# Sixteen pairs of expert visits done 256 columns wide in a mixture-of-experts loop

## Chip, cores and metric

The kernel runs on one core of a Trainium2 chip. The metric is the device time of one execution in microseconds, median of several runs. The engines are named as in the profile: PE (TensorE matmul), PEld (its weight loads), DVE (VectorE), ACT (ScalarE), POOL (GpSimd) and SP (SyncE, which here only issues DMAs).

## What is computed

Two decoder layers over 8 sequences of 128 tokens with 256 features, each with an attention, a cross attention and a feed-forward part, and a layer norm of the sum after each. The part that matters here is the last one, a mixture of 64 experts of which every token uses 8. With 1,024 tokens that makes 8,192 pairs of a token and an expert:

```python
x = hidden_states.reshape(-1, HIDDEN)
logits = jnp.einsum('th,eh->te', x, gate_w)
probs = jax.nn.softmax(logits, axis=-1)
topk_w, topk_idx = jax.lax.top_k(probs, TOP_K)
...
def step(acc, inp):
    w13_e, w2_e, c = inp
    g = x @ w13_e[:INTER].T
    u = x @ w13_e[INTER:].T
    h = jax.nn.silu(g) * u
    o = h @ w2_e.T 
    return (acc + c[:, None] * o, None)
```

`g` and `u` are 128 wide, `o` 256. All of it is fp32. The kernel computes `o` for chosen pairs alone.

## The kernel before

**Order of the pairs.** The pairs are sorted by expert, so that each expert owns a run of columns. `cols` holds the features of the sorted pairs, 128 partitions by 2 halves by 64 blocks of 128 columns and two blocks more. An expert with n pairs takes ceil(n / 128) *visits*, each of 128 columns from a start that is known only at run time. There are at most 127 visits (`NV`); the program has a shorter arm for up to 104 (`FEW`) and chooses by a counted value (L1212 to L1219).

**The routing ahead of the loop.** `choose` takes the best 8 of 64 per token into a mask. `place` counts the pairs of each expert by a matmul with ones (L928 to L930), copies the counts to 128 columns (L935), and multiplies them with a triangle of ones (`before`) to get each expert's first slot (`base`, L937). That is added to the slot numbers (L943). Later, visits per expert are counted (`full`, L991 to L993), summed up to the first visit of each expert (`first`, L994 to L997), and turned into two rows of `visits`: the expert of each visit and its first column (L1049 to L1058). A third row tells the arm. Beside this, DVE and PE turn the slots into one-hot matrices and out of them into `tok_i`, the token of each sorted pair (`locate` and L1029 to L1063). The loop's first gathers wait for `tok_i`.

**The loop, `run_visits`.** One step does one visit v. The order of PE and of POOL is the program's (a manual schedule); the orders of DVE, ACT and SP are the scheduler's.

- `hidden(v)`: PE reads the visit's first column into a register (`begins`, L1119), then 4 fp32 matmuls against gate and up weights, which the profile shows as 8 records of 128 columns (L1150). ACT takes silu of one half (L1158), DVE multiplies with the other (L1160).
- `turn(g)`: PE transposes a gathered block of 128 pairs in two matmuls (L1128) into one of the two PSUM buffers of `ps_tr`, and DVE copies it into `cols` (L1129). `turned(step)` says how many blocks are turned after a step: step + 3 + step // 4, so every fourth step turns two.
- `down(v - 2)`: 2 fp32 matmuls, 4 records (L1167), and ACT copies the result to `cols` over columns that are no longer needed (L1170).
- `fetch(v + 8)`: SP loads the visit's expert, 384 KB, into a ring of 9 tiles (L1138).
- `gather`: POOL gathers blocks by `tok_i`, four ahead of the turned ones, into 6 buffers (L1104).
- `turn_back(g)`: from step 43 on PE transposes a finished block (L1177), DVE copies it (L1179) and POOL scatters it to `pair_rows` in HBM (L1180).
- `weight(b)` and `spread(b)`: DVE work for the tail, in the program every twelfth step; the scheduler puts most of it early.

A block may be used by a visit only once its copy is in `cols`. The visit's first column is at most 128 v, so visit v waits for blocks up to number v.

**The tail.** Eight loads of 1 MB bring the scattered rows back, PE and DVE sum the eight experts of each token with their weights, and a layer norm ends the kernel.

Of the kernel before, what the change touches and what calls it, by code (L numbers as in the profile page):

```python
# [9 lines left out]
F32 = mybir.dt.float32  # L10
# [4 lines left out]
ALU = mybir.AluOpType  # L15
# [22 lines left out]
FEW = 104  # L38
FAR = 65536.0
# [20 lines left out]
def decoder_kernel(ctx: ExitStack, tc: tile.TileContext, i, out):  # L60
# [594 lines left out]
    blks_16 = rp.tile([P, NG, TOP], F16, name="blks_16")  # L655
    comb = rp.tile([P, B, NE], F32, name="combine")
# [20 lines left out]
    def make_constants():  # L677
# [14 lines left out]
        nc.gpsimd.iota(blks_16, pattern=[[1, NG], [0, TOP]], base=0, channel_multiplier=0, allow_small_or_imprecise_dtypes=True)  # L692
        nc.gpsimd.memset(seen[:, 0, :], 0.0)
# [89 lines left out]
    with (  # L783
# [136 lines left out]
        def place(st, b, par):  # L920
# [42 lines left out]
        counts = rp.tile([NE, 2], F32, name="counts")  # L963
        counts_w = rp.tile([NE, P], F32, name="counts_w")
# [34 lines left out]
    lead = rp.tile([NE, 1], F32, name="lead")  # L999
    nc.scalar.activation(lead, first[:, 1:2], AF.Identity, bias=first[:, 0:1], scale=-float(P))  # L1000
    done = rp.tile([NE, 1], F32, name="done")
    nc.scalar.activation(done, first[:, 1:2], AF.Identity, bias=counts[:, 1:2], scale=1.0)
    past = rp.tile([NE, P], F32, name="past")
    nc.gpsimd.tensor_scalar(past, iota[:NE], done, None, ALU.is_ge)
    during = rp.tile([NE, P], F32, name="during")
    nc.gpsimd.tensor_scalar(during, iota[:NE], first[:, 1:2], None, ALU.is_ge)
# [19 lines left out]
    with tc.tile_pool(name="onehot", bufs=3) as op, tc.manual_schedule(engines={nc.vector.engine}):  # L1026
        pn = ps_mm("pair_in").rearrange("p (k g) -> p k g", k=TOP)
        locate(0, 2)
        for b in range(B):  # L1029
# [16 lines left out]
            if b == 0:  # L1046

                px = ps_o("expert_of")[:1, :P]
                nc.tensor.matmul(px, ones[:NE, :1], past, start=True, stop=True)  # L1049
# [6 lines left out]
                nc.gpsimd.tensor_copy(visits[:, 2, :], by_visit[:, 0])  # L1056
# [18 lines left out]
    wring = loop.enter_context(tc.tile_pool(name="wring", bufs=9, side="right"))  # L1075
# [35 lines left out]
    def run_visits(arm, count):  # L1111


# [17 lines left out]
        def fetch(v):  # L1131
# [10 lines left out]
            ws[v] = w  # L1142

        def hidden(v):
            o = begins(v, nc.tensor.engine, fed)
            ps = ps_mm(f"moe_gu_{arm}_{v}")[:, :D].rearrange("p (a t) -> p a t", a=2)
            for a in range(2):
                for k in range(2):
                    at = k * D + a * P
                    mm = nc.tensor.matmul(  # L1150
                        ps[:, a, :], ws[v][:, at : at + P], cols[:, k, bass.ds(o + P, P)],
# [5 lines left out]
            s = mp.tile([P, P], F32, tag="s", name=f"moe_s_{arm}_{v}")  # L1157
            nc.scalar.activation(s, ps[:, 0, :], AF.Silu)  # L1158
            hid = mp.tile([P, P], F32, tag="hid", bufs=4, name=f"moe_h_{arm}_{v}")
            nc.vector.tensor_tensor(hid, ps[:, 1, :], s, ALU.mult)  # L1160
            hs[v] = hid

        def down(v):
            ps = ps_o(f"moe_o_{arm}_{v}")[:, :D].rearrange("p (c t) -> p c t", c=2)
            for c in range(2):
                at = 2 * D + c * P
                nc.tensor.matmul(ps[:, c, :], ws[v][:, at : at + P], hs[v], start=True, stop=True)  # L1167
# [147 lines left out]
```

## Time and profile before

| | |
|---|---|
| median of 3 runs | 881.4 us (881.01 to 885.09) |
| the profiled execution | 886.73 us, span 884.9 us |
| PE busy in the span | 804.7 us (91%) |
| weight loads | 537.0 us (61%) |
| DVE, ACT, POOL busy | 459.7, 289.8, 231.7 us |
| weight loads from HBM in the loop | 104 of 384 KB |
| gathers and scatters | 64 and 64 indirect DMAs |
| first matmul of visit 0 | 639.1 us after the start |
| last start of a down matmul | 843.4 us |

The page gives shares over the whole span. The loop is some 204 us of it, and it has two parts: in the first, blocks are gathered and turned; in the second (about 727 us on), finished blocks are turned back and scattered. The clock that was granted to PE is 1.00 in nearly all of the loop. Records of matmuls overlap, since their ends are modelled; what one costs is read from the distance of starts.

### The profile page before, as it was taken

To read this page: it belongs to the slowest core of one execution; us is meant where nothing else is said; L and a number is where in the kernel's file an instruction comes from. 1 tells how busy PE (TensorE), PEld (TensorE's weight loads), DVE (VectorE), ACT (ScalarE), POOL (GpSimd) and SP (SyncE) were. 2 spreads that over 40 slices of the span, in tenths; PEclk is the share of its full clock that TensorE was granted. 3 is DMA by queue.
4 is the path that set the end of the run, shared out by engine and by line. 5 is a ranking of instruction groups with operands and counts; after the bars stand their busy time and mean duration, and the time that the engine had idled before them with its cause. 6 is when DMAs were issued, how large, how long until landed. Compare 5 with 4: busy or idle time off the path is not lost. (4 is left out here: it accounts for less than half of the span.)

```text
span 884.9 us, 14249 instructions
## 1 busy us (share of the span) xinstructions
PE 804.7 (91%) x4568; PEld 537.0 (61%) x4568; DVE 459.7 (52%) x1280; ACT 289.8 (33%) x994; POOL 231.7 (26%) x321
## 2 busy tenths in 40 slices
PE   7998986999999999999999999996588888999946
PEld 3555553567455558655557755554488877888834
DVE  1899976323544442344444477665795333334326
ACT  2567752221333330133330133332232332333302
POOL 0011113123300000000006121101566655555524
PEclk9999996999999999999999999997599999999979
DMA  6500010730000000000001000000579987989656
GB/s 186 160 1 25 1 49 1 262 119 0 1 0 1 0 1 1 1 0 1 1 1 48 1 7 8 13 13 13 196 227 284 289 273 229 296 294 301 200 205 262
DMA packets 39731, 87.80 MB, mean 99 GB/s; under 512 B 6433, under 2 KB 16193, under 8 KB 38753
## 3 DMA queue, kind: packets, MB, share of 16 engines
q1 hardware_dynamic: 32288, 68.88, 24.0%
q0 software_dynamic: 6144, 16.79, 5.6%
q10 hardware_dynamic: 1216, 1.13, 0.4%
q8 instruction: 41, 0.67, 0.3%
q14 instruction: 42, 0.34, 0.1%
HBM read 76.29 MB, written 10.49 MB: 98 GB/s over the span
## 5 line engine op out<-in xcount | busy, mean ns | idle before, releaser
L228 ACT ACTIVATE l_e<-l_s,nm_l 128x128 f32<-128x128 f32 x256 | 90.2, 370 | 88.7 <-DVE nm_l L225 88.6
L1150 PE MATMUL moe_gu_few<-cols,w_few 128*128 (+1 forms) x832 | 114.6, 281 | 3.7 <-issue 2.3
L1150 PEld LDWEIGHTS moe_gu_few<-cols,w_few 128*128 128x128 f32 x832 | 102.7, 194 | 10.6 <-issue 9.2
L1180 POOL DMA_INDIRECT pair_rows<-moe_os_few,pairs x64 | 63.1, 986 | 55.2 <-DVE moe_os_few L1179 42.9
L1104 POOL DMA_INDIRECT xg_few<-x_rows,tok_i x60 | 62.2, 1037 | 30.8 <-issue 11.9
L1167 PE MATMUL moe_o_few<-moe_h_few,w_few 128*128 128x128 f32 x416 | 63.9, 277 | 0.0
L748 PE MATMUL l_q<-xT_l1a,w_qkv 128*128 128x512 f32 x128 | 60.2, 593 | 0.0
L748 PE MATMUL l_k<-xT_l1a,w_qkv 128*128 128x512 f32 x128 | 60.2, 592 | 0.0
L748 PE MATMUL l_v<-xT_l1a,w_qkv 128*128 128x512 f32 x128 | 60.1, 592 | 0.0
L235 DVE TENSOR_SCALAR l_e<-l_e,inv_l 128x128 f32<-128x128 f32 x256 | 59.3, 295 | 1.2
L851 ACT ACTIVATE y_e<-y_sT 128x512 f32<-128x512 f32 x64 | 33.0, 604 | 81.5 <-PE y_sT L844 48.8
L1170 ACT COPY cols<-moe_o_few 128x256 f32 (+1 forms) x104 | 38.8, 373 | 57.5 <-PE moe_oT_few L1177 21.6
L731 DVE TENSOR_TENSOR l_vs<-l_c,l_vs 128x512 f32<-128x512 f32 x32 | 22.1, 692 | 67.4 <-PE l_c L730 67.4
L711 PE MATMUL l_y<-w_o,l_vs 128*128 128x256 f32 x256 | 56.9, 381 | 0.0
L1158 ACT ACTIVATE moe_s_few<-moe_gu_few 128x128 f32<-128x128 f32 x104 | 29.0, 280 | 80.4 <-PE moe_gu_few L1150 44.8
L1167 PEld LDWEIGHTS moe_o_few<-moe_h_few,w_few 128*128 128x128 f32 x416 | 55.2, 193 | 0.0
L711 PEld LDWEIGHTS l_y<-w_o,l_vs 128*128 128x128 f32 x256 | 48.1, 190 | 9.8 <-issue 2.8
L228 ACT ACTIVATION_READ_ACCUMULATOR l_e<-l_s,nm_l 128x1 f32 x256 | 53.2, 208 | 0.0
L1160 DVE TENSOR_TENSOR moe_h_few<-moe_gu_few,moe_s_few 128x128 f32<-128x128 f32 x104 | 29.8, 287 | 42.2 <-ACT moe_s_few L1158 23.8
L1129 DVE COPY cols<-moe_xT_few 128x256 f32<-128x256 f32 x64 | 26.5, 418 | 47.1 <-PE moe_o_few L1167 23.7
L225 DVE TENSOR_REDUCE nm_l<-l_s 128x4 f32<-128x512 f32 x64 | 43.1, 684 | 10.0 <-PE l_s L763 8.1
L756 ACT COPY l_vs<-l_v 128x512 f32<-128x512 f32 x32 | 18.7, 585 | 78.5 <-PE l_v L748 78.5
(266 smaller groups left out, 1355.8 us busy)
## 6 DMA issues: line engine op xcount, KB each, us to landing
w_few<-in_experts SPq DMA_DIRECT2D x104, 384.0 KB
z<-pair_rows SPq DMA_DIRECT2D x7, 1024.0 KB
w_qkv<-in_w_qkv SPq DMA_DIRECT2D x8, 768.0 KB
w_o<-in_w_o SPq DMA_DIRECT2D x1, 2048.0 KB
xT<-in_xT SPq DMA_DIRECT2D x2, 512.0 KB
x<-in_x SPq DMA_DIRECT2D x4, 256.0 KB
cx<-in_ctx SPq DMA_DIRECT2D x1, 1024.0 KB
q_up<-in_up_qT SPq DMA_DIRECT2D x4, 256.0 KB
```

Of the source, the lines that this page charges most:

```text
L225: nc.vector.tensor_reduce(nm, s, AX.X, ALU.max, negate=True)
L228: nc.scalar.activation(e[:, a, :], s[:, a, :], AF.Exp, bias=nm[:, a : a + 1], scale=1.0, accum_out=sums[:, a : a + 1],)
L235: nc.vector.tensor_scalar(e[:, a, :], e[:, a, :], inv[:, a : a + 1], None, ALU.mult)
L711: nc.tensor.matmul(py[:, :D], scaled[b // 4, m][:, b % 4 * S : (b % 4 + 1) * S], w_o[:, m, :], start=(m == 0), stop=(m == L1_HEADS - 1),)
L748: nc.tensor.matmul(ps, w_qkv[:, k, c, n, :], xT[h][:, k, :], start=(k == 0), stop=(k == 1))
L851: nc.scalar.activation(e, tiles[j], AF.Exp)
L1104: nc.gpsimd.indirect_dma_start(out=x, out_offset=None, in_=xd, in_offset=bass.IndirectOffsetOnAxis(ap=tok_i[:, g : g + 1], axis=0), bounds ...
L1150: mm = nc.tensor.matmul(ps[:, a, :], ws[v][:, at : at + P], cols[:, k, bass.ds(o + P, P)], start=(k == 0), stop=(k == 1),)
L1160: nc.vector.tensor_tensor(hid, ps[:, 1, :], s, ALU.mult)
L1167: nc.tensor.matmul(ps[:, c, :], ws[v][:, at : at + P], hs[v], start=True, stop=True)
L1170: cp = nc.scalar.copy(cols[:, :, bass.ds(o, P)], ps)
L1180: inst = nc.gpsimd.indirect_dma_start(out=zd, out_offset=bass.IndirectOffsetOnAxis(ap=pairs[:, g : g + 1], axis=0), in_=o, in_offset=None, ...
```

## The change

Experts whose number of visits is even are sorted ahead of the others. The first 32 visits are then 16 pairs of one expert each, and a pair is done as one unit: one load of weights, matmuls, silu, product and copy of 256 columns in place of 128. Visits 32 to 103 are units of one visit as before. So the arm has 88 units and 88 loads of weights where it had 104.

For the new order, the experts stand twice on 128 partitions: partitions 0 to 63 count an expert if its number of visits is even, 64 to 127 if it is odd (`even`, `alt`, `keep`). The counts are taken twice, `full` and `first` move ahead into `place`, and `base` is made of `first` by way of `twice`, which folds the two halves. `step_of` undoes the doubling when the expert of a visit is counted. The arm is chosen by two conditions: at least 16 pairs and at most 104 visits. The ring of weights has 8 tiles in place of 9 and is filled 7 units ahead in place of 8; the buffers for silu are 2 of double width in place of 3. In a unit of two visits the loop turns the blocks of both steps one after the other.

```diff
 FEW = 104
+DOUBLES = 16
...
+        for half in range(2):
+            rows = slice(NE * half, NE * (half + 1))
+            nc.gpsimd.memset(even[rows], 1.0 - half)
+            by_two = alt.rearrange("p (j two) -> p j two", two=2)
+            for two in range(2):
+                nc.gpsimd.memset(by_two[rows, :, two], 1.0 if half != two else -1.0)
+        nc.gpsimd.tensor_tensor(twice, ident[:, :NE], ident[:, NE:], ALU.add)
+        nc.gpsimd.tensor_scalar(step_of, ident[:, NE - 1 : NE], -float(NE), 1.0, ALU.mult, ALU.add)
...
-                pc = ps_x("count")[:NE, :1]
-                nc.tensor.matmul(pc, seen[:, b0, :], ones[:, :1], start=True, stop=False)
-                nc.tensor.matmul(pc, flat, ones[:, :1], start=False, stop=True)
+                pc = ps_x("count")[:, :1]
+                for n_src, src in enumerate((seen[:, b0, :], flat)):
+                    for half in range(2):
+                        nc.tensor.matmul(
+                            pc[NE * half : NE * (half + 1)], src, ones[:, :1], start=(n_src == 0), stop=(n_src == 1)
+                        )
             ps = ps_x(f"pos_{b0}")[:, : n * NE]
             nc.tensor.matmul(ps, before, flat, start=True, stop=False)
             nc.tensor.matmul(ps, ones, seen[:, b0 : b0 + n, :].rearrange("p b e -> p (b e)"), start=False, stop=True)
             if last:
-                nc.vector.tensor_copy(counts_w, pc.to_broadcast([NE, P]))
+                nc.vector.tensor_copy(both[:, 0:1], pc)
+                nc.vector.tensor_tensor(full, both[:, 0:1].to_broadcast([P, B]), starts[:, :B], ALU.is_gt)
+                nc.vector.reduce_sum(both[:, 1:2], full, axis=AX.X)
+                nc.vector.tensor_tensor(full, full, alt, ALU.mult)
+                nc.vector.reduce_sum(keep, full, axis=AX.X)
+                nc.vector.tensor_tensor(keep, keep, even, ALU.add)
+                nc.vector.tensor_scalar(counts, both, keep, None, ALU.mult)
+                pf = ps_x("first")[:, :2]
+                nc.tensor.matmul(pf, before, counts, start=True, stop=True)
+                nc.vector.tensor_copy(first, pf)
+                nc.vector.tensor_scalar(counts_w, ones, first[:, 0:1], keep, ALU.mult, ALU.mult)
                 pb = ps_x("base")[:, :NE]
-                nc.tensor.matmul(pb, counts_w, before[:NE, :NE], start=True, stop=True)
+                nc.tensor.matmul(pb, counts_w, twice, start=True, stop=True)
...
-                nc.vector.tensor_copy(counts[:, 0:1], counts_w[:, 0:1])
...
-    full = rp.tile([NE, B], F32, name="full")
-    nc.vector.tensor_tensor(full, counts[:, 0:1].to_broadcast([NE, B]), starts[:NE, :B], ALU.is_gt)
-    nc.vector.reduce_sum(counts[:, 1:2], full, axis=AX.X)
-    pf = ps_o("first")[:NE, :2]
-    nc.tensor.matmul(pf, before[:NE, :NE], counts, start=True, stop=True)
-    first = rp.tile([NE, 2], F32, name="first")
-    nc.scalar.copy(first, pf)
...
-                nc.tensor.matmul(px, ones[:NE, :1], past, start=True, stop=True)
+                nc.tensor.matmul(px, step_of, past, start=True, stop=True)
                 pv = ps_tr("visit")[:1, :P]
                 nc.tensor.matmul(pv, lead, during, start=True, stop=True)
                 by_visit = rp.tile([1, 2, P], F32, name="by_visit")
                 nc.scalar.copy(by_visit[:, 0], px)
                 nc.scalar.copy(by_visit[:, 1], pv)
                 nc.gpsimd.tensor_scalar(visits[:, 0, :], by_visit[:, 0], float(NE - 1), None, ALU.min)
-                nc.gpsimd.tensor_copy(visits[:, 2, :], by_visit[:, 0])
+                pq = ps_o("enough")[:1, :2]
+                for n_at, at in enumerate((2 * DOUBLES - 1, FEW)):
+                    nc.tensor.matmul(pq[:, n_at : n_at + 1], ones[:, :1], past[:, at : at + 1], start=True, stop=True)
+                ended = rp.tile([1, 2], F32, name="ended")
+                nc.scalar.copy(ended, pq)
+                nc.gpsimd.tensor_scalar(ended[:, 0:1], ended[:, 0:1], float(NE), None, ALU.is_lt)
+                nc.gpsimd.tensor_scalar(visits[:, 2, 0:1], ended[:, 0:1], ended[:, 1:2], None, ALU.mult)
...
-    wring = loop.enter_context(tc.tile_pool(name="wring", bufs=9, side="right"))
+    wring = loop.enter_context(tc.tile_pool(name="wring", bufs=8, side="right"))
...
-    def run_visits(arm, count):
+    def run_visits(arm, count, doubles):
+        units = [(2 * j, 2) for j in range(doubles)] + [(v, 1) for v in range(2 * doubles, count)]
...
-        def fetch(v):
+        def fetch(u):
+            v = units[u][0]
...
-            ws[v] = w
-        def hidden(v):
+            ws[u] = w
+        def hidden(u):
+            v, width = units[u]
+            n = width * P
             o = begins(v, nc.tensor.engine, fed)
-            ps = ps_mm(f"moe_gu_{arm}_{v}")[:, :D].rearrange("p (a t) -> p a t", a=2)
+            ps = ps_mm(f"moe_gu_{arm}_{v}")[:, : 2 * n].rearrange("p (a t) -> p a t", a=2)
             for a in range(2):
                 for k in range(2):
                     at = k * D + a * P
                     mm = nc.tensor.matmul(
-                        ps[:, a, :], ws[v][:, at : at + P], cols[:, k, bass.ds(o + P, P)],
+                        ps[:, a, :], ws[u][:, at : at + P], cols[:, k, bass.ds(o + P, n)],
                         start=(k == 0), stop=(k == 1),
                     )
 
                     tc.declare_no_dep(mm.ins, group=f"left_{arm}", reason="columns of earlier visits")
             fed.append(mm.ins)
-            s = mp.tile([P, P], F32, tag="s", name=f"moe_s_{arm}_{v}")
+            s = mp.tile([P, 2 * P], F32, tag="s", bufs=2, name=f"moe_s_{arm}_{v}")[:, :n]
             nc.scalar.activation(s, ps[:, 0, :], AF.Silu)
-            hid = mp.tile([P, P], F32, tag="hid", bufs=4, name=f"moe_h_{arm}_{v}")
+            hid = mp.tile([P, 2 * P], F32, tag="hid", bufs=4, name=f"moe_h_{arm}_{v}")[:, :n]
             nc.vector.tensor_tensor(hid, ps[:, 1, :], s, ALU.mult)
-            hs[v] = hid
-        def down(v):
-            ps = ps_o(f"moe_o_{arm}_{v}")[:, :D].rearrange("p (c t) -> p c t", c=2)
+            hs[u] = hid
+        def down(u):
+            v, width = units[u]
+            n = width * P
+            ps = ps_o(f"moe_o_{arm}_{v}")[:, : 2 * n].rearrange("p (c t) -> p c t", c=2)
             for c in range(2):
                 at = 2 * D + c * P
-                nc.tensor.matmul(ps[:, c, :], ws[v][:, at : at + P], hs[v], start=True, stop=True)
+                nc.tensor.matmul(ps[:, c, :], ws[u][:, at : at + P], hs[u], start=True, stop=True)
             o = begins(v, nc.scalar.engine, left)
 
-            cp = nc.scalar.copy(cols[:, :, bass.ds(o, P)], ps)
+            cp = nc.scalar.copy(cols[:, :, bass.ds(o, n)], ps)
...
-            for step in range(-8, count + 4):
-                if 0 <= step < count:
-                    hidden(step)
-                for g in range(turned(step - 1), turned(step)):
+            ahead_of = 7
+            for u in range(-ahead_of, len(units) + 4):
+                if u < 0:
+                    lo, hi = u, u + 1
+                elif u < len(units):
+                    lo, hi = units[u][0], sum(units[u])
+                else:
+                    lo, hi = count + u - len(units), count + u - len(units) + 1
+                if 0 <= u < len(units):
+                    hidden(u)
+                for g in range(turned(lo - 1), turned(hi - 1)):
                     turn(g)
-                if 0 <= step - 2 < count:
-                    down(step - 2)
-                if 0 <= step + 8 < count:
-                    fetch(step + 8)
-                while len(xg) < min(turned(step) + 4, NG):
+                if 0 <= u - 2 < len(units):
+                    down(u - 2)
+                if 0 <= u + ahead_of < len(units):
+                    fetch(u + ahead_of)
+                while len(xg) < min(turned(hi - 1) + 4, NG):
                     xg[len(xg)] = gather(len(xg), arm)
-                if 0 <= step - 3 - spare < NG:
-                    turn_back(step - 3 - spare)
-                if 0 <= step < 12 * B and step % 12 == 11:
-                    weight(step // 12)
-                    spread(step // 12)
+                for g in range(max(lo - 3 - spare, 0), min(hi - 3 - spare, NG)):
+                    turn_back(g)
+                for step in range(max(lo, 0), hi):
+                    if step < 12 * B and step % 12 == 11:
+                        weight(step // 12)
+                        spread(step // 12)
...
-        visits[0:1, 2, FEW : FEW + 1], min_val=0, max_val=NE,
+        visits[0:1, 2, 0:1], min_val=0, max_val=P,
         skip_runtime_bounds_check_because="a number of experts",
     )
-    with tc.If(few == NE) as enough:
-        run_visits("few", FEW)
+    with tc.If(few == P) as enough:
+        run_visits("few", FEW, DOUBLES)
     with enough.Else():
-        run_visits("all", NV)
+        run_visits("all", NV, 0)
```

More of the change, by code (lines that the diff above doesn't have):

```diff
@@ L655, in decoder_kernel @@
     blks_16 = rp.tile([P, NG, TOP], F16, name="blks_16")
+    alt = rp.tile([P, B], F32, name="alt")
+    even = rp.tile([P, 1], F32, name="even")
+    twice = rp.tile([P, NE], F32, name="twice")
+    step_of = rp.tile([P, 1], F32, name="step_of")
     comb = rp.tile([P, B, NE], F32, name="combine")
@@ L961, in place @@
                 )
-        counts = rp.tile([NE, 2], F32, name="counts")
-        counts_w = rp.tile([NE, P], F32, name="counts_w")
+        both = rp.tile([P, 2], F32, name="both")
+        full = rp.tile([P, B], F32, name="full")
+        keep = rp.tile([P, 1], F32, name="keep")
+        counts = rp.tile([P, 2], F32, name="counts")
+        first = rp.tile([P, 2], F32, name="first")
+        counts_w = rp.tile([P, P], F32, name="counts_w")
         def finish_heads(step):
@@ L989, in decoder_kernel @@
     nc.gpsimd.memset(cols[:, :, (NG + 1) * P :], 0.0)
-    full = rp.tile([NE, B], F32, name="full")
-    nc.vector.tensor_tensor(full, counts[:, 0:1].to_broadcast([NE, B]), starts[:NE, :B], ALU.is_gt)
-    nc.vector.reduce_sum(counts[:, 1:2], full, axis=AX.X)
-    pf = ps_o("first")[:NE, :2]
-    nc.tensor.matmul(pf, before[:NE, :NE], counts, start=True, stop=True)
-    first = rp.tile([NE, 2], F32, name="first")
-    nc.scalar.copy(first, pf)
-    lead = rp.tile([NE, 1], F32, name="lead")
+    lead = rp.tile([P, 1], F32, name="lead")
     nc.scalar.activation(lead, first[:, 1:2], AF.Identity, bias=first[:, 0:1], scale=-float(P))
-    done = rp.tile([NE, 1], F32, name="done")
+    done = rp.tile([P, 1], F32, name="done")
     nc.scalar.activation(done, first[:, 1:2], AF.Identity, bias=counts[:, 1:2], scale=1.0)
[L1003 to L1006, printed above, removed]
+    past = rp.tile([P, P], F32, name="past")
+    nc.gpsimd.tensor_scalar(past, iota, done, None, ALU.is_ge)
+    during = rp.tile([P, P], F32, name="during")
+    nc.gpsimd.tensor_scalar(during, iota, first[:, 1:2], None, ALU.is_ge)
     nc.gpsimd.tensor_tensor(during, during, past, ALU.subtract)
```

## Prediction

> **What bounds it now.** I first read the stages by windows. The rows hold start and end, length, then busy time and instructions of PE, weight loads, DVE, ACT and POOL, the granted clock, the DMA share and GB/s.
>
> ```profile
> 632.00:640.00 8.00, 2.05 (x8) 1.45 (x9) 3.35 (x7) 0.00 (x0) 6.17 (x7) 0.50 0.80 290
> 640.00:670.00 30.00, 26.35 (x215) 24.57 (x215) 29.27 (x93) 9.13 (x27) 21.21 (x19) 0.98 0.74 229
> 670.00:702.00 32.00, 28.57 (x245) 27.06 (x243) 11.44 (x37) 9.80 (x33) 19.94 (x20) 1.00 0.90 285
> 744.00:841.00 97.00, 92.72 (x756) 85.04 (x755) 38.11 (x107) 32.26 (x106) 52.30 (x54) 1.00 0.84 269
> ```
>
> The visits fill 639 to 843 us of 884.9. PE and DMA both look nearly full, so neither share decides. The timeline of PE does, over four visits of the stretch that the change touches:
>
> ```profile
> 689.70 0.44 PE L1128 MATMUL moe_xT_few<-ident,xg_few 128*128 128x128 f32 x2 [0.91 <-issue]
> 689.98 0.61 PE L1167 MATMUL moe_o_few<-moe_h_few,w_few 128*128 128x128 f32 x4
> 690.42 1.06 PE L1150 MATMUL moe_gu_few<-cols,w_few 128*128 x8
> 691.32 0.38 PE L1128 MATMUL moe_xT_few<-ident,xg_few 128*128 128x128 f32 x2
> 691.53 0.61 PE L1167 MATMUL moe_o_few<-moe_h_few,w_few 128*128 128x128 f32 x4
> ...
> 694.43 0.95 PE L1128 MATMUL moe_xT_few<-ident,xg_few 128*128 128x128 f32 x4
> 695.22 0.61 PE L1167 MATMUL moe_o_few<-moe_h_few,w_few 128*128 128x128 f32 x4
> 695.67 1.06 PE L1150 MATMUL moe_gu_few<-cols,w_few 128*128 x8
> 697.67 0.44 PE L1128 MATMUL moe_xT_few<-ident,xg_few 128*128 128x128 f32 x2 [0.94 <-issue]
> ```
>
> A record of eight starts 0.90 us before its successor (690.42 to 691.32): 0.112 us per matmul. A transposed block (two records) costs 0.21. So four visits are 4 x 12 x 0.112 + 5 x 0.21 = 6.43 us of work in a period of 697.67 - 689.70 = 7.97; 1.54 is waiting, 0.9 of it ahead of a second transpose in one step. What that transpose waits for is on DVE:
>
> ```profile
> 689.22 0.42 DVE L1129 COPY cols<-moe_xT_few 128x256 f32<-128x256 f32 x1 [1.90 <-PE moe_gu_few L1150]
> 689.57 0.28 DVE L1160 TENSOR_TENSOR moe_h_few<-moe_gu_few,moe_s_few 128x128 f32<-128x128 f32 x1
> 689.76 0.84 DVE L1129 COPY cols<-moe_xT_few 128x256 f32<-128x256 f32 x2
> ...
> 693.94 0.42 DVE L1129 COPY cols<-moe_xT_few 128x256 f32<-128x256 f32 x1 [3.13 <-PE moe_o_few L1167]
> ```
>
> The copy ends at 689.64 and PE goes on at 689.70: the two PSUM buffers of `ps_tr` were full. The copy itself was late. The block transposed at 691.32 to 691.70 is copied only from 693.94, 2.24 us later, though DVE stood idle for 3.13 us. Where PE stops, the copies come 0.43 us after (PE ends at 688.80, the copy starts at 689.22). I can't name what holds PE's signal while PE streams; I take its size from these rows.
>
> Two more views settle what is *not* the bound: PE's idle time around the weight tiles, and the waits of SP's queue.
>
> ```profile
>   issue: 11.4, 34
>   ACT moe_s_few L1158: 0.8, 1
>   DVE diag L1095: 0.5, 1
> ```
>
> ```profile
> SPq L1138 <- PE moe_gu_few L1150: 44.0, 35, 1.8
> SPq L1138 <- PE moe_o_few L1167: 22.2, 15, 2.3
> ```
>
> No wait of PE was ended by a landing of `w_few`; SP waits for PE to give ring slots back. The 16 loads that go (16 x 393 KB = 6.3 MB, 22 us at the 285 GB/s of the row) are hidden work, and I book nothing for them.
>
> **PE's work in the first 32 visits.** Now 32 x 12 x 0.112 = 43.0, plus 39 blocks (the formula of `turned` from 2 to 41) x 0.21 = 8.2: 51.2 of the 62.4 us between the first matmuls of visits 0 and 32 (639.13 and 701.51 in the timeline). 11.2 are waits. For 256 columns in fp32 the page has a row:
>
> ```profile
> L711 PE MATMUL l_y<-w_o,l_vs 128*128 128x256 f32 x256 | 56.9, 381 | 0.0
> ```
>
> 56.9 / 256 = 0.222 us, twice 0.112. Sixteen pairs are 16 x 12 x 0.222 = 42.6, with the blocks 50.8: the half as many weight loads save PE 0.4 us. The Trainium skill says otherwise: its page "TensorE: Matmul & The Clock Gate", section "Back-to-back issue gap", has a stream of load and matmul pairs at about 81 ns for 128 columns and 131 for 512. As an estimate from that page, 256 columns would cost 1.2 times 128 columns and the pairs would be 17 us cheaper, some 867 us in all; the row of this case shows 2.0 times, so the measurement decides.
>
> **Waits after the change.**
> (a) A pair turns two or three blocks at once; by the formula units 2, 4, ... 14 turn three. The third needs the buffer of the first, with only 0.21 us of PE work between. As PE then stops, I price it by the stop above, 0.91: 7 x 0.91 = 6.4. Bounds: 0.25 if the copy starts at once (0.42 + 0.05 - 0.21), 2.5 if it comes 2.24 late.
> (b) A pair reads two blocks, so the cover between turning a block and using it falls by one visit. Units 1, 2 and 4 need a block turned just before them. For 1 and 2 no down projection stands between: 0.43 + two copies 0.84 + 0.05 = 1.3 each; unit 4 has one, I take 0.9. Sum 3.5; bounds 1.0 (copies at once) and 6.
> (c) The slow first matmuls (2.08 for eight at a clock of 0.50, against 0.90) stay: 1.2.
> (d) DVE is full until 670 (29.27 of 30.00) with the weight and diagonal work, and a copy waits for half an instruction of 0.68: 3 x 0.35 = 1.0; bounds 0 and 2.
> Sum: 50.8 + 6.4 + 3.5 + 1.2 + 1.0 = 62.9, against 62.4: +0.5.
>
> **Ahead of the loop.** After the last count DVE does seven small dependent operations where one copy of 0.28 stood. Dependent ones follow each other after 0.20 (own_at 618.22, blk 618.42): 1.4 - 0.28 = +1.1. A matmul and its copy now stand in the chain (`first`: counts done at 618.04, its copy at 618.51): +0.5, and two short DVE operations +0.4. Cover: `counts_w` was ready at 615.46 and its matmul started at 616.11 behind the position matmuls, -0.65. The two operations on `full` leave DVE later, -0.1. Sum +1.3 (bounds 0.6 and 2.0). All that follows on DVE, the one-hots, `tok_i` and the gathers, moves with it. The first pair needs two blocks: the second copy ends at 639.65, the first visit began at 639.13: +0.5 (0 to 0.7). POOL's nine added constants stand where POOL is idle. Its two tiny operations on `ended` replace a cast of 0.82; SP's first fetch at 624.80 has 14 us until its use, and were that gone they would cost under 1 us.
>
> **Beside the path.** Silu, product and copy become one instruction of double width for two: 0.37, 0.42 and 0.59 (rows of those widths) for 2 x 0.28, 2 x 0.29 and 2 x 0.37, all shorter. SP and the register loads have 16 fewer. POOL needs 5 gathers at 1.30 (1.00 and 0.30 of issue) = 6.5 per two pairs of about 7.2, hidden with 0.7 left; were it gone, POOL would set the period at 6.5, below the forecast. The ring has 8 tiles for 9: a fetch runs a visit (1.8 us) later against its use. The 37th fetch is issued by 699.9 and its visit starts at 709.4, so 9.5 us shrink to 7.7.
>
> **Sum.** +0.5 + 1.3 + 0.5 = +2.3 us on the profiled execution, which took 886.73 (span 884.9); the median of the runs is 881.4. I carry the difference over: 883.7 us. About 0.5% (4.4 us) is what a measurement can tell, so the forecast is no change.
>
> **Rivals.**
> *Faster, the signals come in time.* If the transfers' pressure (0.90 busy) or the many short matmuls hold the signals back, 16 fewer loads and half the matmuls release them. With the lower bounds: 50.8 + 1.8 + 1.0 + 1.2 = 54.8, -7.6 + 0.6 = 874.4; with no wait but the slow start 52.0, -10.4 + 0.6 = 871.6. For it: outside this loop copies follow matmuls at once. Against: the waits come from two PSUM buffers, which stay two. Chance 0.25.
> *Slower, the third turn is late for the next unit as well.* If signals are held for a number of matmuls, twice as wide ones hold them twice as long. The third block's copy is then not done when the next unit's second block wants its buffer, one more stop of 0.91 for each of 7: +6.4, 890.1. It decides from 4.4 - 2.3 = 2.1 us of added waiting, 0.3 per two pairs. For it: the 2.24 us against only 4 x 0.222 + 8 x 0.222 = 2.66 of PE work in between, with a copy of 0.42 still to come. Against: a stop frees what is held. At the upper bound of (a), 7 x 1.6 more, 895. Chance 0.32.
> *It does something else.* If fewer than 16 pairs exist, the program takes the other arm: 127 visits at 1.9 are 23 x 1.9 = +44 us, 925. The reference's routing on its own inputs gives 103 visits, 36 of them of experts with an even number, so this needs an error. With a ring that runs dry, 0.03.
>
> **Numbers.** No change 0.40, faster 0.25, slower 0.35. The time is that of the forecast, 883.7; its own range, with (a) between 0.5 and 1.3, is 880 to 887. The range over all, 873 to 892, takes in both first rivals and leaves out their far ends.
>
> **What would show it.** First matmul of the loop at 640.9; 16 pairs in 63 us; eight gate and up matmuls of a pair in 1.78; a stop of about 0.9 ahead of every third turn. The forecast is wrong if the pairs take under 57 us (faster rival) or over 65 (slower), if the per-matmul time at 256 columns is not 0.22, or if PE waits for `w_few`.

## The result, and the profile after

| | before | after |
|---|---|---|
| median, 8 runs each on one chip | 882.80 us (880.53 to 885.09) | 886.73 us (885.15 to 890.27) |
| ratio after to before | | 1.0052, 95% interval 1.0031 to 1.0074 |
| profiled execution, span | 886.73 us, 884.9 | 889.62 us, 887.9 |
| last mask to the loop's first matmul | 24.42 us | 24.00 us |
| first 32 visits (after: 16 pairs) | 62.38 us | 62.17 us |
| visits 32 to 103 | 142.14 us | 140.96 us |
| bytes in the queue of the weight loads | 68.88 MB | 62.59 MB |

The kernel became 3.9 us slower (2.7 to 6.5 by the interval). The windows of the pairs and of the single visits behind them (start and end, length, then busy time and instructions of PE, weight loads, DVE, ACT and POOL, granted clock, DMA share, GB/s) are, in the kernel before,

```profile
639.10:701.50 62.40, 55.31 (x455) 52.00 (x455) 41.34 (x130) 18.75 (x59) 41.74 (x40) 0.98 0.81 256
701.50:843.60 142.10, 130.13 (x1045) 119.20 (x1044) 55.77 (x161) 45.72 (x149) 78.28 (x80) 0.99 0.82 263
```

and in the kernel after:

```profile
643.50:705.70 62.20, 52.06 (x262) 43.64 (x263) 40.77 (x117) 15.00 (x30) 45.56 (x43) 0.98 0.58 169
705.70:846.70 141.00, 127.98 (x1045) 119.52 (x1043) 54.21 (x158) 46.41 (x146) 78.41 (x80) 0.99 0.82 263
```

The number of matmuls falls from 455 to 262 and the DMA share from 0.81 to 0.58, and the stretch is as long as it was. The timeline of PE in the kernel after shows the steady state of a pair of units:

```profile
690.74 1.89 PE L1187 MATMUL moe_gu_few<-cols,w_few 128*128 x8
692.47 0.60 PE L1162 MATMUL moe_xT_few<-ident,xg_few 128*128 128x128 f32 x4
694.05 0.44 PE L1162 MATMUL moe_xT_few<-ident,xg_few 128*128 128x128 f32 x2 [0.98 <-DVE cols L1163]
694.32 1.03 PE L1206 MATMUL moe_o_few<-moe_h_few,w_few 128*128 128x256 f32 x4
695.19 1.89 PE L1187 MATMUL moe_gu_few<-cols,w_few 128*128 x8
```

Eight gate and up matmuls go from 690.74 to 692.47, 0.216 us each: about twice the time of a narrow one (0.112) for twice the columns. Then two blocks are turned, and the third stands 0.98 us for DVE's copy. The list of PE's waits over the 16 pairs (sum, times, longest) has nothing else but the early copies (the first of these three, 0.52 us, still stands ahead of the first gate matmul):

```profile
PE moe_xT_few L1162 <- DVE cols L1163: 8.3, 7, 1.9
PE moe_gu_few L1187 <- DVE cols L1163: 2.3, 3, 1.2
```

If pairs, single visits and the way into the loop are all a little shorter, where are 3 us more? They are there before the last mask is made: it ends at 614.71 us before and at 619.55 after. Part of that is one place, at 228 us, hundreds of microseconds ahead of the loop. The timeline of all engines (start, length, what it was idle for and on whom) shows, before,

```profile
225.71 4.12 POOL L695 TENSOR_SCALAR keys<-cx,quarter,one_row 128x2048 f32<-128x2048 f32 x2
...
226.80 3.29 DVE L235 TENSOR_SCALAR l_e<-l_e,inv_l 128x128 f32<-128x128 f32 x4
...
230.15 0.70 PE L730 MATMUL l_c<-l_e,ones 128*128 128x512 f32 x1 [0.70 <-DVE l_e L235]
```

and after:

```profile
227.27 0.09 POOL L702 MEMSET even<- 64x1 f32 x1
...
228.10 0.19 POOL L708 TENSOR_SCALAR step_of<-ident 128x1 f32<-128x1 f32 x1
...
228.37 4.10 POOL L711 TENSOR_SCALAR keys<-cx,quarter,one_row 128x2048 f32<-128x2048 f32 x2
...
228.48 4.44 DVE L236 TENSOR_SCALAR l_e<-l_e,inv_l 128x128 f32<-128x128 f32 x4
...
232.98 0.70 PE L746 MATMUL l_c<-l_e,ones 128*128 128x512 f32 x1 [1.86 <-DVE l_e L236]
```

Before, POOL starts its two `keys` instructions 1.09 us ahead of DVE's four `l_e`; after, 0.11 us ahead, because the eight instructions for the new constants stand in POOL's queue in front of them. The four instructions of DVE then take 4.44 us in place of 3.29, and PE waits 1.86 in place of 0.70. (The next four, with POOL done, take 0.88 at 234.68.) That is 1.15 us. The rest, 3.7 us, stands where the program is the same in both. The row of the cross attention's first matmul before,

```profile
L820 PE MATMUL y_s<-keys,x 32*128 32x512 f32 x128 | 36.6, 642 | 1.7 <-ACT r_e L952 1.7
```

and after:

```profile
L836 PE MATMUL y_s<-keys,x 32*128 32x512 f32 x128 | 38.1, 674 | 1.7 <-ACT r_e L982 1.7
```

The same 128 matmuls take 1.5 us longer. Most of them take 640 ns in both profiles; those that start between 580 and 590 us take 640 ns before and 909 ns in the mean after, and there the granted clock is lower, 0.83 after against 0.91 before in the mean of 575 to 595 us. The mean granted clock of the whole execution is 0.952 after and 0.959 before. Such losses lie at 17, 135, 548 and 580 us of the profiled execution.

The account of the two profiled executions: +1.15 (constants) + 3.69 (same code, lower clock) - 0.42 (routing) - 0.21 (pairs) - 1.18 (visits 32 to 103) - 0.05 (tail) = +2.98; the spans differ by 3.0. Why visits 32 to 103, done one by one in both kernels, took 1.18 us less isn't shown.

### The profile page after: what moved, and what is told of

It reads as the page before. It is cut to its first block, busy times and chain, and to the rows that moved or that the text cites. A ratio compares the mean times of both kernels' runs of the same rounds, so it can differ in the third digit from the quotient of the medians.

```text
span 887.9 us, 13620 instructions
## 1 busy us (share of the span) xinstructions
PE 804.6 (91%) x4384; PEld 531.8 (60%) x4384; DVE 459.7 (52%) x1269; ACT 287.3 (32%) x962; POOL 233.0 (26%) x330
## 3 DMA queue, kind: packets, MB, share of 16 engines
q1 hardware_dynamic: 29984, 62.59, 21.8%
q10 hardware_dynamic: 1216, 1.13, 0.4%
## 4 chain that ended last, share of the span: by engine, by line
PE 68%; DVE 14%; issue 5%; POOL 5%; DMA 4%; ACT 3%; another core or an unknown queue 0%; SPq 0%; POOLq 0%; ACTq 0%; DVEq 0%
PE moe_gu_few L1187 7%; PE l_y L727 6%; PE l_q L764 6%; PE l_k L764 6%; PE l_v L764 6%; PE y_s L836 4%; PE up L321 4%; POOL pair_rows L1219 3%; PE l_s L779 3%; PE l_c L746 3%; PE down L334 3%; PE moe_o_few L1206 3%; DVE l_e L236 3%; DMA z<-pair_rows 3%; PE y_av L879 2%
## 5 line engine op out<-in xcount | busy, mean ns | idle before, releaser
L1187 PE MATMUL moe_gu_few<-cols,w_few 128*128 (+1 forms) x704 | 111.2, 301 | 5.0 <-DVE cols L1163 2.3
L1187 PEld LDWEIGHTS moe_gu_few<-cols,w_few 128*128 128x128 f32 x704 | 95.9, 194 | 14.6 <-issue 7.6
L1137 POOL DMA_INDIRECT xg_few<-x_rows,tok_i x60 | 64.1, 1068 | 25.6 <-issue 11.6
L1206 PE MATMUL moe_o_few<-moe_h_few,w_few 128*128 128x128 f32 (+1 forms) x352 | 60.8, 296 | 0.0
L1209 ACT COPY cols<-moe_o_few 128x256 f32 (+2 forms) x88 | 36.3, 413 | 60.0 <-PE moe_o_few L1206 22.7
L1195 ACT ACTIVATE moe_s_few<-moe_gu_few 128x128 f32<-128x128 f32 (+1 forms) x88 | 26.2, 298 | 78.3 <-PE moe_gu_few L1187 40.5
L1206 PEld LDWEIGHTS moe_o_few<-moe_h_few,w_few 128*128 128x128 f32 x352 | 49.3, 193 | 0.8
L1197 DVE TENSOR_TENSOR moe_h_few<-moe_gu_few,moe_s_few 128x128 f32<-128x128 f32 (+1 forms) x88 | 27.5, 313 | 38.6 <-ACT moe_s_few L1195 20.7
```

The costliest lines, as they stand in the source:

```text
L1137: nc.gpsimd.indirect_dma_start(out=x, out_offset=None, in_=xd, in_offset=bass.IndirectOffsetOnAxis(ap=tok_i[:, g : g + 1], axis=0), bounds ...
L1187: mm = nc.tensor.matmul(ps[:, a, :], ws[u][:, at : at + P], cols[:, k, bass.ds(o + P, n)], start=(k == 0), stop=(k == 1),)
L1206: nc.tensor.matmul(ps[:, c, :], ws[u][:, at : at + P], hs[u], start=True, stop=True)
L1209: cp = nc.scalar.copy(cols[:, :, bass.ds(o, n)], ps)
```

## The experiments

Three groups of four kernels ran, each group on a chip of its own beside the kernel before. On these chips the kernel before takes 859.6, 858.2 and 859.2 us, 23 to 25 us less than on the chip of the first comparison, and the difference lies in the loop. So totals are compared inside a group only.

### Group one: what costs ahead of the loop, and do loads count?

The constants alone:

```diff
 (before) make_constants, ahead of keys
+        for half in range(2):
+            ...
+        nc.gpsimd.tensor_scalar(step_of, ident[:, NE - 1 : NE], -float(NE), 1.0, ALU.mult, ALU.add)
```

> The kernel before, with the nine added POOL constants alone, in the place they have in the change; nothing reads them. Theory (they push the two keys instructions on POOL 1.1 us later, over the whole of DVE's four l_e instructions, which slow down beside them): +1.1 us on before, the row of four DVE l_e instructions at 4.4 us in place of 3.3. Rival (POOL is idle there and nothing waits for it): 0.0, and l_e stays at 3.3 us.

Measured: 861.68 against 859.63 us, ratio 1.0015 (0.9997 to 1.0033). The total leaves both theories standing; the timeline doesn't:

```profile
226.16 4.42 DVE L235 TENSOR_SCALAR l_e<-l_e,inv_l 128x128 f32<-128x128 f32 x4
```

The constants behind the keys:

```diff
 (after) make_constants
+        (seen and keys)
         (even, alt, twice, step_of)
-        (seen and keys)
```

> The kernel after, with the same nine constants issued behind the two keys instructions in place of ahead of them. Theory: 1.1 us below the kernel after, so +2.8 us on before, l_e back at 3.3 us. Rival (free work): as the kernel after, +3.9 us on before. A third outcome, worse than after, if a layernorm's POOL instructions wait behind the constants.

Measured: 863.88 us, ratio 1.0058 (1.0038 to 1.0077), 4.25 us above before, so the total missed the 2.8 and lies nearer the rival's 3.9. The row is as the theory has it:

```profile
225.89 3.28 DVE L236 TENSOR_SCALAR l_e<-l_e,inv_l 128x128 f32<-128x128 f32 x4
```

Five of its six runs took 863.5 to 865.3 us, and the profiled one 856.93. What differs between executions is seen by laying each profile's instructions beside those of the first profile of before (how much later, in us, at four times of that profile):

| kernel | constants ahead of keys | 220 us | 240 us | 540 us | 612 us |
|---|---|---|---|---|---|
| b_const | yes | -0.64 | 0.49 | 0.48 | 2.26 |
| a_single | yes | -0.92 | 0.21 | 0.21 | 1.92 |
| after_again | yes | -0.37 | 0.77 | 0.76 | 2.57 |
| a_tr3 | yes | -0.64 | 0.49 | 0.49 | -3.72 |
| a_late | no | -0.91 | -0.92 | -0.92 | -5.04 |
| a_best | no | -1.03 | -1.04 | -1.04 | -0.99 |
| b_hold | no | 2.35 | 2.36 | 2.35 | 2.48 |
| b_noload | no | -0.63 | -0.63 | -0.64 | 1.35 |

From 220 to 240 us every kernel with the constants ahead of the keys loses 1.13 to 1.15 us (the first profile of after too: 1.68 to 2.83), and the others nothing. From 540 to 612 us, in code that is the same in all, executions differ by -4.2 to +2.0. So the 1.15 is shown, and a total of one kernel moves by several microseconds for a reason that has nothing to do with the edit.

The new routing with the old loop:

```diff
 (after)
-        run_visits("few", FEW, DOUBLES)
+        run_visits("few", FEW, 0)
```

with a ring of 9, eight ahead, and tiles of single width.

> The kernel after with its sorting of the experts, but 104 visits of one each, 104 loads, a ring of nine and eight loads ahead: the loop of before behind the new routing. Theory (what the change costs lies ahead of the loop): constants 1.1 plus the chain from the last mask to tok_i 1.7, +2.8 us on before, the loop's 32 first visits at 62.4 us as before. Rival (the start of the loop follows from the burst of weight loads and not from tok_i): the 1.7 is swallowed by the 8-load burst, +1.1 us. Rival (the order of the experts itself costs): over +4.

Measured: 863.60 us, ratio 1.0055 (1.0036 to 1.0075). In the profile, the last mask to `tok_i` takes 18.00 us against 16.24 in the kernel with the constants alone: +1.76. But the loop's first matmul comes 23.29 us after the mask against 24.36: 1.07 *sooner*. The rival was right, the later `tok_i` is swallowed, and more. The 32 visits take 57.65 us against 56.66. The total, 4.0 us above before, comes nearest to the last expectation (over 4), and the profile has no place for that much: an order of experts that costs 1.0 in the 32 visits, and 1.15 for the constants, less 1.07. Losses of clock as in the table could make up the rest; in which of its runs they fell isn't seen.

One load for two narrow visits:

```diff
 (a_single) fetch
+            if v < shared and v % 2:
+                ws[u] = ws[u - 1]
+                return
```

> As the kernel with single visits behind the new routing, but the 16 pairs share one load each: 88 loads, all matmuls 128 columns wide. Theory (the loads are hidden behind PE): the 32 first visits take as long as with 104 loads within 0.5 us; the first matmul of the loop may come up to 2.7 us sooner, since only four loads and not eight stand ahead of the first gathers; so 0 to -2.7 us against single visits with 104 loads. Rival (the loads crowd the DMA and hold gathers up all through the pairs): 3 to 6 us less in the 32 visits themselves.

Measured: 862.04 us, ratio 1.0036 (1.0019 to 1.0053). The 32 visits take 57.78 us against 57.65: there the loads were hidden. The loop starts at 23.22 after the mask; the burst was not halved, since SP filled all nine tiles at once again.

### Group two: what holds PE in the pairs?

> The kernel after, unchanged, once more, so that the other runs of this group have it beside them. Theory (the cost lies ahead of the loop): ratio to before 1.003 to 1.006 on any chip; the loop's first 16 pairs take as long as the 32 visits of before within 2 us, whichever length both have here.

Measured: 865.75 us against 858.17, ratio 1.0087 (1.0054 to 1.0119), higher than expected. The pairs take 58.56 us; the 32 visits of before take 56.35 in the kernel of this group whose loads are left out below (56.66 with the constants alone, in group one). So on these chips the pairs are 2 us longer than the single visits of before, and the 72 visits behind them 120.1 us (121.4 with the constants alone).

Three banks (PSUM buffers) for turns:

```diff
-    open_banks()
+    open_banks(3, 3)
```

> The kernel after, with three banks for the turns and three for the gate/up results from the routing on, in place of two and four. Theory (before every third turn PE stands for DVE's copy, 0.9 to 1.9 us each in the profile of after, because only two banks take turns): about 7 stops less, the 16 pairs 5 to 8 us shorter than in the kernel after. Rival (the stop only moves to the next wait, that of the gate/up matmuls for their bank or of down for the hidden tile): 0 to 2 us.

Measured: 860.52 us, ratio 1.0026 (0.9999 to 1.0053); the pairs 54.82 us, 3.7 less than in the unchanged kernel after of the same group, less than the 5 to 8 that were taken from the first chip. PE's waits over the pairs, in that kernel,

```profile
PE moe_xT_few L1162 <- DVE cols L1163: 4.7, 7, 1.8
PE moe_gu_few L1187 <- DVE cols L1163: 2.3, 3, 1.2
```

and with three banks:

```profile
PE moe_gu_few L1187 <- DVE cols L1163: 2.2, 3, 1.2
PE moe_xT_few L1162 <- DMA xg_few<-x_rows,tok_i: 0.8, 1, 0.8
```

The seven stops go, 4.7 us here and not 8.3, and a wait for a gather of 0.8 comes: 3.9.

PE without register loads:

```diff
 (before) hidden
-            o = begins(v, nc.tensor.engine, fed)
+            o = min(v, NG) * P
```

> The kernel before, with PE's gate/up matmuls reading columns at fixed places, so that PE loads no register in the loop; the columns read are not those of the visit where experts end within a block, so the result isn't the reference's. Theory (PE's register loads and addresses hold up its signals, which come 0.6 to 1.6 us late in the mean in the profile of before): signals from gate/up to the silu 0.1 us or less in the mean, the 32 first visits 4 to 6 us and the other 72 up to 17 us shorter than before on a chip where the signals are late. Rival (transfers or the chip itself hold them up): the lags as in the other runs of this group, the loop shorter by no more than 72 of the 0.22 us stops for a register, 8 us at the most.

Measured: 856.30 us, ratio 0.9965 (0.9943 to 0.9988); the 32 visits 54.56 us. On this chip PE's signals are prompt in every kernel, so the run can't tell what makes them late on the first. The 32 visits are 1.8 us shorter (54.56 against 56.35), but the 72 behind them are not (118.6 against 117.8 in the kernel whose loads are left out below). PE's waits for DVE's copies in the 32 visits are 0.3 us here and 2.3 us there, so the 1.8 isn't shown to be the register loads' own time.

Later visits with the first nine visits' weights:

```diff
 (before) fetch
+            if v >= 9:
+                ws[v] = ws[v % 9]
+                return
```

> The kernel before, with only the first nine visits' weights loaded; all later visits use those again, so the result isn't the reference's and 37 MB less are moved. Theory of registers: PE's signals as late as in the other runs of this group, the loop within 2 us. Rival (the transfers hold up PE's signals): the lags fall to 0.1 us, the 104 visits up to 20 us shorter on a chip where signals are late. On a chip with prompt signals neither shows more than 3 us, but the gathers come sooner.

Measured: 856.85 us, ratio 0.9965 (0.9940 to 0.9989); the 32 visits 56.35 us. With 95 loads of 104 gone, the first 32 visits are only 0.3 us shorter than with all of them in group one (56.66). The 72 behind them take 117.8 us, where the other kernels on these chips take 118.6 to 121.7; so the loads are shown to be hidden in the first 32 visits alone.

### Group three: single visits with the same help, and the start of the loop

> The kernel before, with three banks for the turns and three for the gate/up results from the routing on, in place of two and four. Theory (PE stands before every fifth turn of the visits as it does in the pairs): 2 to 3 us less in the 32 first visits where PE's signals are prompt, 4 to 6 us where they are late; ratio to before about 0.997. Rival (the stop moves to the next wait): within 0.5 us of before. The 16 pairs with three banks took 54.8 us; if the 32 single visits with three banks take 54.8 us or less, the pairs bring nothing in themselves.

(The edit is that of three banks above, in the kernel before.) Measured: 859.03 us, ratio 0.9999 (0.9981 to 1.0017); the 32 visits 55.60 us, about 1 us less than 56.35 and 56.66. Single visits have fewer stops to lose: PE waits three times for DVE's copies of a turn, 2.3 us in all, in the kernel with the constants alone, and once, 0.5 us, here. PE did not stand before every fifth turn, as the theory had it.

Loads held behind the first gathers:

```diff
 (before)
...
+    with tc.issue_after(gathers[1].ins):
+        nc.gpsimd.tensor_copy(experts_again, visits[:, 0, :])
...
 fetch
-                    visits[0:1, 0, v : v + 1], engines=[nc.sync.engine], ...
+                    (experts_again if v >= HELD else visits[:, 0, :])[0:1, v : v + 1], engines=[nc.sync.engine], ...
```

> The kernel before, with the fifth and later weight loads held until the first four gathers are issued (their table is copied once more on POOL behind the gathers). Theory (the burst of eight or nine loads, and not tok_i, sets the start of the loop, since the gathers land behind it): from the last mask to the first matmul of the loop 22.0 us in place of 24.4, and 2.0 to 2.4 us less on the whole. Rival (tok_i and the gathers' own way set the start): 24.4 as before and no gain; or the held loads come late and give it back at visits 4 to 8.

Measured: 857.99 us, ratio 0.9981 (0.9958 to 1.0003). From the last mask to the loop 21.49 us, and 24.45 in the kernel with three banks alone on the same chip. The timeline shows why. In the kernel before, the first gather is issued at 631.28 and PE turns its block 6.67 us later:

```profile
631.28 1.31 POOL L1104 DMA_INDIRECT xg_first<-x_rows,tok_i  x1 [6.24 <-DMA w_few<-in_experts]
...
637.95 0.66 PE L1128 MATMUL moe_xT_few<-ident,xg_first 128*128 128x128 f32 x2 [7.93 <-DMA xg_first<-x_rows,tok_i]
```

With the held loads it is 3.17 us later:

```profile
633.73 1.32 POOL L1106 DMA_INDIRECT xg_first<-x_rows,tok_i  x1 [6.21 <-DMA w_few<-in_experts]
...
636.90 0.45 PE L1130 MATMUL moe_xT_few<-ident,xg_first 128*128 128x128 f32 x1 [4.43 <-DMA xg_first<-x_rows,tok_i]
```

and in the kernel after it is 3.22 us later without any help, since there the gather is issued when most loads have landed:

```profile
637.87 1.32 POOL L1137 DMA_INDIRECT xg_first<-x_rows,tok_i  x1 [9.65 <-DMA w_few<-in_experts]
...
641.09 0.45 PE L1162 MATMUL moe_xT_few<-ident,xg_first 128*128 128x128 f32 x1 [4.48 <-DMA xg_first<-x_rows,tok_i]
```

So the theory of the burst holds. Only about half of its gain seems to stay: the 32 visits then take 57.98 us. From the last mask to visit 32 it is 79.5 us, against 80.9 and 81.0 in the kernel without the later loads and in the one with the constants alone, on the other two chips. The total is 1.2 us below before, where 2.0 to 2.4 were expected.

Both edits in the kernel before, and all three (constants, banks, held loads) in the kernel after:

> The kernel before with both: three banks for turns, and the held loads. Theory: the two gains add, 4 to 5 us below before (ratio about 0.995). Rival: the earlier start only meets the next wait, no more than the larger of the two gains.

> The kernel after with the constants behind the keys, three banks for turns and the held loads. Theory: 1.1 (constants) + 3.7 (stops) + 0.3 (in the change the gathers leave so late that the burst is nearly over) = 5.1 us below the kernel after, about as long as before or 1 us less, and 3 to 5 us above the kernel before with the same two edits. Rival (pairs pay once the stops are gone): as fast as before with the two edits, or faster.

Measured: 857.31 us, ratio 0.9972 (0.9954 to 0.9991), and 858.63 us, ratio 0.9995 (0.9971 to 1.0018). The first is faster than before by 0.8 to 4.0 us, the only version that computes everything of which that can be said; its interval and the second's overlap. So neither forecast came: the two gains don't add to 4 or 5 us, and the second is 1.3 us above the first and not 3 to 5. The loop of the first starts 3.0 us sooner than with three banks alone (21.48 against 24.45 after the mask), but its 32 visits take 58.52 us against 55.60, which gives 2.9 back. Its list of PE's waits over these visits says to whom:

```profile
PE moe_xT_few L1130 <- DMA xg_few<-x_rows,tok_i: 3.0, 4, 0.9
```

PE now runs ahead of the gathers. From the last mask to visit 32 the first takes 80.00 us and the kernel with three banks alone 80.05: here the held loads bring nothing, and the profile doesn't show where the total gained. The pairs of the second take 55.61 us, but its loop starts 23.98 us after the mask, as without the held loads (24.00). From the mask to the end of the pairs that is 79.59 us: with the stops gone, pairs and single visits on the same chip are equal to half a microsecond.

## Why the prediction was right, and where it wasn't

The forecast was 883.7 us, +2.3 on the profiled execution; measured were 886.73 and +3.9 (2.7 to 6.5). The time lies inside the forecast's own range of 880 to 887, and the ratio on the 0.5% that was taken as the bound of no change. That the size of the loss fits to 1.6 us is luck, though. The three terms of the +2.3 were +0.5 for the pairs, +1.3 for the chain ahead of the loop and +0.5 for its second block. Measured were -0.21 for the pairs and -0.42 for the whole way from the last mask into the loop. What made the profiled execution longer stands in none of the terms: 1.15 us for the constants and 3.69 at a lower clock.

**PE's work, and the loads: right.** 0.222 us per 256 columns was forecast and 0.216 measured. That fp32 matmuls cost by columns is why the pairing takes away half the matmul instructions and no time, and the estimate of 867 us from the Trainium skill, "TensorE: Matmul & The Clock Gate", "Back-to-back issue gap", doesn't apply. That loads are hidden in these visits is shown by the kernel with one load for two narrow visits (57.78 against 57.65).

**The stops: right in place, and in sum by errors that cancel.** Seven third turns at 6.4 and the early units at 3.5, with 1.0 for a crowded DVE: 10.9 forecast. Measured were 8.3 for the third turns and 1.8 for the early units (2.3 less the 0.52 ahead of the first gate matmul), 10.1. Unit 4 waited for no early copy, where 0.9 was forecast, and the third turns cost 1.9 more than 6.4. Taking two banks' limit away removes them (4.7 us on the other chip). The pairs took 62.2 us for 62.9. The rival "slower" wanted a second stop for every third turn; the list has seven in all. Two of them are longer. At unit 6 (1.7 us) DVE was busy all the time from 666.0 to 670.7 us; at unit 8 (1.9 us) it stood idle for 3.26 us until PE's signal came.

**The faster rival: its condition came, its time did not.** On the other chips PE's signals are prompt: the copy follows the turn at once. In the kernel with the constants alone, PE's turn at 690.87 ends at 691.25 and DVE's copy starts at 691.29:

```profile
690.87 0.38 PE L1141 MATMUL moe_xT_few<-ident,xg_few 128*128 128x128 f32 x2
691.09 0.61 PE L1180 MATMUL moe_o_few<-moe_h_few,w_few 128*128 128x128 f32 x4
```

```profile
691.29 0.42 DVE L1142 COPY cols<-moe_xT_few 128x256 f32<-128x256 f32 x1 [0.94 <-PE moe_xT_few L1141]
```

There the pairs still take 58.5 us: prompt signals help single visits more (62.4 to 56.7 us) than pairs (62.2 to 58.5), and the pairs keep 6.5 us of waits. With the same new order of experts, on the chip of group one, the pairs take 58.5 and the single visits 57.7 us. On the first chip itself the condition came in part: from the last gate matmul to the silu it is 1.42 us in the mean over the first 32 visits before, and 0.40 over the 16 pairs. The rival compared pairs with prompt signals to visits with late ones.

**"POOL's nine added constants stand where POOL is idle": wrong, 1.15 us.** They are eight instructions. POOL's own idle time was counted, not the engine that runs beside the instructions queued behind: the later `keys` hold DVE up for longer, as the last section shows. All six profiles with the constants ahead of the keys show it, at 1.13 to 1.15 us (the one-load kernel goes from -0.48 to 0.66), and none of the others.

**The chain ahead of the loop, +1.3, and the second block, +0.5: the first right in size and without effect.** Mask to `tok_i` grew by 1.74 (16.27 to 18.01), yet the loop starts 0.42 sooner after the mask. A cover wasn't seen. The gathers of before wait behind the burst of weight loads, 6.67 us from issue to use against 3.22, so a later `tok_i` cost nothing. The burst itself ends sooner, too: its first load leaves 8.90 us after the mask in place of 10.09. Of these 1.19 us, some 0.4 come from `first`, which is ready sooner (its first reader on ACT starts 3.60 us after the mask in place of 3.98), and 0.7 from POOL, whose `during` takes 0.68 us in place of 1.39. Against that, the second gathered block is now the one waited for: from the first turn to the first gate matmul 2.46 us in place of 1.18, +1.28 where +0.5 was forecast. In sum +1.74 - 3.45 + 1.28 = -0.43.

**Not forecast at all: the clock, 3.7 us of the profiled difference,** in code that the change doesn't touch. Whether the change makes such losses more frequent stays open: the four experiments with the new routing and two banks lie 2.4 to 7.6 us above before in their medians, more than their profiles have a place for. The granted clocks on record point the same way: over all runs of a kernel, the mean is 0.953 to 0.955 in the six kernels of the experiments with the new routing, and 0.955 to 0.957 in the six with the old one and in the kernel before beside them; all eight runs of the first comparison with the change have 0.951 to 0.955. But where in an execution the clock is lower only a profile shows. With one profile of each kernel, and one of these 7 us below its kernel's other runs, this isn't settled.

What holds PE's signals on the first chip also stays open: register loads and transfers were tried on a chip that doesn't have the effect.

## What to carry to other kernels

Halving the instructions of a matmul stream gains nothing where a matmul's time follows its columns; look first at the waits that the new grouping makes, here a third turn with two banks. A step added to an idle engine still moves what is queued behind it; look at who runs beside *that*. And a longer chain is free only as long as another one, here the burst of loads, ends later: find the later of the two before either is priced.

## What the runs showed of the hardware

**The same program runs its loop 20 us faster on other chips.** The 72 single visits, with equal instructions, take 142.1 us on the first chip and 121.4 on another:

```profile
698.00:819.40 121.40, 118.17 (x1046) 116.33 (x1044) 55.30 (x159) 47.57 (x146) 77.83 (x80) 1.00 0.89 308
```

The clock is as high (0.99 and 1.00), but the signal from the last gate matmul to the silu takes 0.59 us in the mean and 2.9 at most on the first chip, and 0.04 always on the other. The faster chip has the higher DMA share (0.89 against 0.82), which speaks against the transfers as such as what makes signals late; it isn't shown.

**DVE stands for POOL, instruction by instruction.** The view of one tile's instructions gives each its least, median and largest time in ns. In the kernel after:

```profile
L236 DVE TENSOR_SCALAR l_e<-l_e,inv_l x4: 275/1148/2122, 228.5 to 232.6; 128x128 f32<-128x128 f32 x4
```

```profile
L711 POOL TENSOR_SCALAR keys<-cx,quarter,one_row x2: 2052/2056/2059, 228.4 to 230.4; 128x2048 f32<-128x2048 f32 x2
```

Two of the four take 2.0 and 2.1 us, and end 0.07 and 0.08 us after the two of POOL, which keep their 2.05. The other two take 0.28. Before, the first came 1.09 us into a `keys` and took 1.03 us, to 0.08 after its end; the third met the other (1.91). The Trainium skill, "SBUF — State Buffer", "Who interferes with whom", has this rule: a DVE `tensor_scalar` in a mode that takes two ports and a POOL instruction take turns, the one that is first keeps the ports for its whole length and the other is fully blocked. These rows agree with the blocking, though no view shows the mode of the `l_e`; it was the rule to weigh against "idle".

**A register load on PE** takes 0.30 us on its sequencer (the median of 103 in the kernel before). Without them the first 32 visits are 1.8 us shorter and the 72 behind them are not.
